# A two-layer graph network on one core: normalising and projecting the first node groups ahead of the rest

## The chip, the cores and the metric

The kernel runs on one core of a Trainium2 chip. The metric is the device time of one launch, in microseconds; of several runs the median is given. Engines are named as in the profile: PE (matrix products and transposes; PEld is its weight load), DVE, ACT and POOL (elementwise engines), and SP, which only issues DMAs. ACT and POOL issue DMAs too, each through a queue of its own; an engine that issues a DMA does nothing else meanwhile.

## The reference, cut to what matters

There are n = 3327 nodes with d = 128 features each, an adjacency matrix of 3327 x 3327, and H = 8.

```
h = relu(layernorm(x))                          # over the 128 features
deg = adj.sum(1);  deg[deg == 0] = 1
g = (adj.T @ h / deg) @ W_n.T + b_n + h @ W_c.T + b_c
x = x + relu(gamma * batchnorm(g) + beta)       # batch norm: over the nodes

h = relu(layernorm(x))
q = (h @ Wq.T).reshape(d, n, H)                 # the same for k and v
a = einsum('dnh,dmh->dnm', q, k) * d**-0.5 + adj + adj
o = einsum('dnm,dmh->dnh', softmax(a, axis=2), v)
x = x + o.reshape(n, H * d) @ Wo.T
```

The reshape to (d, n, H) cuts the row-major result of n x 1024 into 128 batches of 3327 rows with 8 columns. Attention is done on 128 batches, each with 3327 x 3327 scores. One node gives 128 rows, so 104 nodes (13312 rows) cover four batches (13308 rows).

## The kernel before, in words

**Layer 0.** x lies in SBUF as `xs`, 128 partitions x 26 chunks (NC) x 128 features, node c*128+p on partition p. The adjacency comes in 26 blocks of rows; PE gathers them into eight PSUM banks (`acc`, the last block of 512 nodes shorter), while ACT and DVE sum and take maxima. Then follow the division by the degree, the products with `wn`, and the batch-norm statistics, which end in `scale` and `shift`. `A` then holds the layer's value with features on partitions.

**Between the layers** (lines 615 to 722, written out by hand in program order, one list that each engine runs in its own order). `parts` are chunk ranges: part 0 is chunk 0, part 1 chunks 1 to 3, the others four chunks each. For a part, `relu` (ACT, L620) applies batch norm, `residual` turns it with PE (L626) and adds it to `xs` on DVE (L634), `measure` takes layernorm statistics on DVE (L638, L640), `roots` is a square root on ACT (L381), `factors` two small DVE operations that give `rs` and `mr`; `second_norm` (L646, L651) applies them, and `columns` turns the result with PE and takes the relu into `B`, features on partitions (L659, L661). Part 0 is taken through all this first, as the first 104 nodes are projected at once: `projections` with `quick` true makes six parts (k, q, v, two halves of 512 columns each). A projection of k or q is split into a rounded value and its remainder, `o[:, 0]` and `o[:, 1]`, so that products at reduced precision keep their accuracy. Each is stored twice (`L245`, four DMAs for each half, 208 KB each): `qT` and `kT` in DRAM have 4*H = 32 rows, in the order in which a product of 32 rows pairs value and remainder. The other parts follow; at the end all columns go to `hd` in DRAM (L665), and `xs` to `xd` (L722), from where later groups read them.

**Attention** (`attention`, L764). There are 32 groups (NG) of four batches (G). A group has a tile set: `k` and `q` with 32 partitions for each batch, and `v`. `first_loads` fills set 0: k is read from `kT` into the `k` tile of set 1 as a staging area `ks`, four DMAs, two on SP and two on ACT (L943), q's first 512 columns likewise, then adjacency tiles `at` and weight tiles `wt` through `fetch` (L836, L826), then v. Seven copies on ACT, DVE and POOL sort k from the staging order (L956; a chunk's elements are 26 apart there, 104 bytes). The other sets are filled during the group before, by `loads`: k in two halves through a tile `ks`, 14 sorts on POOL (L190), and q.

The queries of a group are cut into seven blocks y. Strings of tokens (WIDE, NARROW, LAST) give the order of work in a block:
- `A` (`plain`): two PE products (L851) into one of three PSUM buffers, and on DVE the sum with the adjacency (L972) into `d`. Four fill one `d` tile.
- `B` (`weighted`): two products, the exponential on ACT into `f` (L991), the product with weights `wt` on POOL (L992).
- `L`: the exponential of a full `d` tile on ACT (L910).
- `v`: eight matmuls with v into `av` (`second`, L725), six tokens behind; here, too, DMAs and small work are put in: `loads`, `more_weights` (group 0 alone: a tile `t` is read at L870, its exponential stored as weights), `further`, and in group 0 the list `others` (q's remaining columns, L1048).
- `P`, `E`: the start and the middle of one part of `extra`: the projections of a later group (through `further`: `hj`, 104 columns, is read from `hd`, L890), or the output of an earlier one (`outputs`, which reads `xj` from `xd`). There are two P in a wide block, 12 in a group.

Pools that are closed leave their space to the pools of attention, in order of address: so the first `f` tile lies on the old `xs`, and its first use waits for the store of `xs`.

Of the kernel before, what the change touches and what calls it, by code (L numbers as in the profile page):

```python
# [18 lines left out]
N = 3327  # L19
# [16 lines left out]
RUN = 4  # L36
HEAVY = (2, 6, 10, 14, 18, 21)
# [19 lines left out]
def tile_two_layer_gnn(  # L57
# [33 lines left out]
    qT = dram.tile([4 * H, TP], F32, name="qT")  # L91
    kT = dram.tile([4 * H, TP], F32, name="kT")
# [7 lines left out]
    xd = dram.tile([P, NC, D], F32, name="xd")  # L100
    hd = dram.tile([P, NP], F32, name="hd")
# [30 lines left out]

    def tile_set(qkp, x):
        k = qkp.tile([P, NC, P], F32R, name=f"k{x}")
        q = qkp.tile([P, NP], F32R, name=f"q{x}")
        v = qkp.tile([P, G, NC, H + 1], F32, name=f"v{x}")

        nc.vector.memset(v[96:, :, NC - 1, :], 0.0)
        return q, k, v
# [4 lines left out]
    def q_load(q, p0, d, n0=0, n=NP):  # L144

        return (
            q[p0 : p0 + 4 * H, n0 : n0 + n].bitcast(F32), qT[:, bass.ds(d * N + n0, n)]
        )

    def k_load(k, p0, d, n0=0, n=NP):  # L150
        return k[p0 : p0 + 4 * H].bitcast(F32), kT[:, bass.ds(d * N + n0, n)]
# [13 lines left out]
    def loads(tiles, d, ksp):  # L165
# [9 lines left out]
        qs = [dma(*q_load(q, 32 * b, batch(b))) for b in range(G)]  # L175
        vv = [dma(*a) for a in v_loads(v, d)]
        todo = []
        for half in range(2):
# [3 lines left out]
                dma(*k_load(ks, 32 * b, batch(b), half * (NP // 2), NP // 2))  # L182
                for b in range(G)
            ]
            todo += vv if half == 0 else []
            for c in range(0, NC, 4):
                n = min(4, NC - c)

                def sort(ks=ks, c=c, n=n, half=half):
                    nc.gpsimd.tensor_copy(  # L190
                        k[:, c : c + n, half * 64 : half * 64 + 64],
                        ks.bitcast(F32).rearrange("g (p c) -> g c p", c=NC)[:, c : c + n, :],
                    )

                todo.append(sort)
                if c % 8 == 4 and qs:
                    todo.append(qs.pop(0))
# [4 lines left out]
    def projection(wk, hj, j, s, e, quick, ov, factor, queue):  # L202
# [8 lines left out]
        if s == 2:  # L211
            nc.vector.tensor_copy(
# [28 lines left out]
        for a in range(2):  # L241
            for i in range(2):
                g = ((a, i), (i, a))[s]
                g = (2 * g[0] + g[1]) * H + e * (H // 2)
                queue[i].dma_start(  # L245
                    (qT, kT)[s][g : g + H // 2, tok].rearrange("g (p u) -> p g u", u=D),
                    of[:CH, a].rearrange("p (h u) -> p h u", u=D),
                )

    def projections(wk, hj, j, quick, ov, factor, queues=((nc.sync, nc.sync),) * 3):  # L250
# [3 lines left out]
        ]  # L254

    def outputs(wk, j):
# [7 lines left out]
        for c in range(j * CH // P, ((j + 1) * CH - 1) // P + 1):  # L264
            m0, m1 = max(j * CH, c * P), min((j + 1) * CH, (c + 1) * P)
            nc.sync.dma_start(
                xj[m0 - j * CH : m1 - j * CH], xd[m0 - c * P : m1 - c * P, c, :]
            )
# [38 lines left out]
    with tc.tile_pool(name="l0", bufs=1) as l0, tc.tile_pool(  # L307
        name="l0adj", bufs=4
    ) as ap, tc.tile_pool(name="l0s", bufs=4) as sp, tc.tile_pool(
        name="l0w", bufs=1  # L310
    ) as lw, tc.tile_pool(name="l0last", bufs=1) as ll, tc.tile_pool(name="l0p", bufs=1, space=PSUM) as pp:


        xs = ll.tile([P, NC, D], F32, name="xs")
        A = l0.tile([P, NC, D], F32, name="A")
        B = ll.tile([P, NC, P], F32, name="B")
        C = l0.tile([P, NC, P], F32, name="C")
        A2, B2, C2 = (t.rearrange("p c d -> p (c d)") for t in (A, B, C))
        junk = l0.tile([P, N], mybir.dt.bfloat16, name="junk")
        deg = l0.tile([P, NC], F32, name="deg")  # L320
        rdeg = l0.tile([P, NC], F32, name="rdeg")
        wn = l0.tile([P, D], F32, name="wn")
        wc = l0.tile([P, D], F32, name="wc")
        cols = l0.tile([P, 4], F32, name="cols")
        bias = l0.tile([P, 1], F32, name="bias")
# [12 lines left out]
        def load(c):  # L338

            a = ap.tile([P, 7 * NB], F32, name="a")  # L340
# [17 lines left out]
        root = l0.tile([P, 1], F32, name="root")  # L358
# [6 lines left out]
        st = l0.tile([P, NC, 6], F32, name="ln_st")  # L365
        mv = l0.tile([P, NC, 2], F32, name="ln_mv")
        sd = l0.tile([P, NC], F32, name="ln_sd")
        rs = l0.tile([P, NC], F32, name="ln_rs")
        mr = l0.tile([P, NC], F32, name="ln_mr")
# [86 lines left out]
        top = l0.tile([P, 1], F32, name="top")  # L456
        b = l0.tile([1, 6], F32, name="bound")
# [45 lines left out]
        for c in range(NC):  # L503
# [17 lines left out]
            def reduce():  # L521
                nc.scalar.activation(  # L522
                    junk, a[:, :N], AF.Copy, accum_out=deg[:, c : c + 1]
# [30 lines left out]
        a = ap.tile([P, 7 * NB], F32, name="a")  # L554
# [7 lines left out]
        bst = l0.tile([P, NQ, 6], F32, name="bn_st")  # L562
        bmv = l0.tile([P, 2], F32, name="bn_mv")
        scale = l0.tile([P, 1], F32, name="bn_scale")
        shift = l0.tile([P, 1], F32, name="bn_shift")
# [63 lines left out]
        def bank_of(i):  # L629
            return acc[max(0, i - 1)]  # L630
# [11 lines left out]
        def second_norm(i, engine=None):  # L642

            for c in range(*parts[i]):
                if engine is None:
                    nc.scalar.activation(  # L646
                        C[:, c, :], xs[:, c, :], AF.Relu,
                        bias=mr[:, c : c + 1], scale=rs[:, c : c + 1],
                    )
                else:  # L650
                    engine.tensor_scalar(  # L651
                        C[:, c, :], xs[:, c, :], rs[:, c : c + 1], mr[:, c : c + 1],
                        ALU.mult, ALU.add,
                    )

        def columns(i, scalar):
            pt, cs = turned_part(i, C, bank_of(i))
            if scalar:
                nc.scalar.activation(B[:, cs, :], pt, AF.Relu)  # L659
            else:  # L660
                nc.vector.tensor_scalar(B[:, cs, :], pt, 0.0, None, ALU.max)  # L661

        def keep_columns(c0, c1):
            cs = slice(c0 * P, c1 * P)
            nc.gpsimd.dma_start(hd[:, cs], B2[:, cs])  # L665

# [4 lines left out]
        roots(0, 1)  # L671
        factors(0, 1)
        second_norm(0, nc.vector)
        columns(0, True)
        relu(2)
        now = projections(
            sp, B2[:, :CH], 0, True, ov, low_half[:CH, 1:2],
            ((nc.scalar, nc.gpsimd), (nc.sync, nc.gpsimd), (nc.gpsimd,)),
# [14 lines left out]
        residual(1)  # L693
        project(1)
        relu(3)
        measure(1)
        multiply(2, 3)
        residual(2)
        project(2)
        measure(2)  # L700
        project(3)
        relu(4)
        multiply(4, 5)
        relu(5)
        relu(6)
        relu(7)
        project(4, 5)
        for i in range(3, len(parts)):
            residual(i)
            measure(i)  # L710
        roots(1, NC)

        nc.scalar.activation(root, eps, AF.Exp)
        factors(1, NC)
        for i in range(1, len(parts)):
            second_norm(i, (nc.vector, nc.gpsimd, None)[i % 3])
        for i in range(1, len(parts)):
            columns(i, i % 3 != 0)
            if i == 4:
                keep_columns(0, 16)  # L720
        keep_columns(16, NC)
        nc.gpsimd.dma_start(xd, xs)  # L722

# [40 lines left out]
    def attention():  # L764
# [3 lines left out]
        with tc.tile_pool(name="exd", bufs=3) as ep, tc.tile_pool(  # L768
            name="qk1", bufs=1
        ) as qkp1, tc.tile_pool(name="adj", bufs=4) as ap, tc.tile_pool(  # L770
            name="adw", bufs=3
        ) as wp, tc.tile_pool(name="exf", bufs=6) as fp, tc.tile_pool(
# [8 lines left out]
            for av in avs2:  # L781
                nc.vector.memset(av, 0.0)
# [61 lines left out]
            def product(i, y, c, half):  # L844
                q, k, _ = sets[i % 2]
                n0, w = qblocks[y]
# [13 lines left out]
                q_load(sets[0][0], 32 * b, b, NB, NP - NB) for b in range(G)  # L860
            ]

            def more_weights(i, y, v):

                if i or y + 1 >= NY or v not in (2, 16, 24):
                    return
                n0, w = qblocks[y + 1]
                if v == 2:
# [12 lines left out]
            extra, begun, then = [], [], []  # L881

            def further(i, y, v):

                if v == 6:
                    for j in [1, 2] if i == 0 else [i + 2] if i + 2 < NG else []:
                        if y != (2 * (j - 1) if i == 0 else 0):
                            continue
                        hj = wk.tile([P, CH], F32, name="hj")
                        nc.sync.dma_start(hj, hd[:, j * CH : (j + 1) * CH])  # L890
                        extra.extend(projections(wk, hj, j, False, ov, low_half[:CH, 1:2]))
# [44 lines left out]
            def first_loads():  # L936

                q, k, v = sets[0]
                ks = sets[1][1].rearrange("p c n -> p (c n)")
                for load, tile_, n in ((k_load, ks, NP), (q_load, q, NB)):  # L940
                    for b in range(G // 2):
                        for x, queue in ((b, nc.sync), (b + 2, nc.scalar)):
                            queue.dma_start(*load(tile_, 32 * x, x, 0, n))  # L943
                fetch(0, 4)
                fetch(1, 0)
# [3 lines left out]
                for c, copy in (  # L949
                    (16, nc.scalar.copy), (0, nc.vector.tensor_copy),  # L950
                    (4, nc.gpsimd.tensor_copy), (8, nc.scalar.copy),
                    (20, nc.vector.tensor_copy), (12, nc.gpsimd.tensor_copy),
# [306 lines left out]
```

## Time and profile before

| | us |
|---|---|
| median of 3 runs | 9930.07 (9927.71 to 9933.09) |
| the profiled execution | 9923.27 |
| its span, first to last instruction | 9921.5 |
| PE, DVE, ACT, POOL busy | 9328.9, 9260.4, 9762.9, 8406.5 |
| mean granted PE clock | 0.994 |

Busy shares are means over the whole span. The layers differ: layer 0 ends at about 212 us, attention runs from about 262 us to the end, and what lies between is short and has limits of its own. Sums by stretch and the timelines of single engines tell more of it than the page.

### The profile page before, as it was taken

To read this page: it belongs to the slowest core of one execution; us is meant where nothing else is said; L and a number is where in the kernel's file an instruction comes from. 1 tells how busy PE (TensorE), PEld (TensorE's weight loads), DVE (VectorE), ACT (ScalarE), POOL (GpSimd) and SP (SyncE) were. 2 spreads that over 40 slices of the span, in tenths; PEclk is the share of its full clock that TensorE was granted. 3 is DMA by queue.
4 is the path that set the end of the run, shared out by engine and by line. 5 is a ranking of instruction groups with operands and counts; after the bars stand their busy time and mean duration, and the time that the engine had idled before them with its cause. 6 is when DMAs were issued, how large, how long until landed. Compare 5 with 4: busy or idle time off the path is not lost. (4 is left out here: it accounts for less than half of the span.)

```text
span 9921.5 us, 180311 instructions
## 1 busy us (share of the span) xinstructions
PE 9328.9 (94%) x71535; PEld 2846.0 (29%) x71535; DVE 9260.4 (93%) x8949; ACT 9762.9 (98%) x5375; POOL 8406.5 (85%) x4084
## 2 busy tenths in 40 slices
PE   7899999999999999999999999999999999999998
PEld 3222222222222222222222222222222222222222
DVE  5899999999999999999999999999999999999998
ACT  5999999999999999999999999999999999999999
POOL 2788888888888888888888888888888888888887
PEclk9999999999999999999999999999999999999999
DMA  7765556665566665566655566655566656666554
GB/s 302 219 194 174 176 173 185 179 180 172 172 181 186 180 177 171 174 181 183 181 176 174 173 184 181 181 175 172 175 184 184 179 167 176 179 185 181 164 158 130
DMA packets 1132126, 1789.64 MB, mean 180 GB/s; under 512 B 95558, under 2 KB 464196, under 8 KB 1121924
## 3 DMA queue, kind: packets, MB, share of 16 engines
q1 hardware_dynamic: 1127071, 1760.22, 59.7%
q8 instruction: 561, 9.19, 0.4%
q10 hardware_dynamic: 2772, 12.06, 0.3%
q0 software_dynamic: 1424, 5.73, 0.2%
q14 instruction: 298, 2.43, 0.1%
HBM read 1620.90 MB, written 156.76 MB: 179 GB/s over the span
## 5 line engine op out<-in xcount | busy, mean ns | idle before, releaser
L972 DVE SCALAR_TENSOR_TENSOR d<-at,s 128x1024 f32<-128x1024 f32 x7488 | 8693.6, 1216 | 509.3 <-PE s L851 255.7
L992 POOL TENSOR_TENSOR f<-f,wt 128x1024 f32<-128x1024 f32 x3328 | 7875.6, 2395 | 1273.8 <-ACT f L991 1270.0
L910 ACT ACTIVATE d<-d 128x4096 f32<-128x4096 f32 (+1 forms) x1888 | 6931.6, 3671 | 1.3 <-DVE av L743 0.4
L851 PE MATMUL s<-q,k 32*128 32x512 f32 x23296 | 3939.7, 464 | 488.8 <-ACT f L991 261.7
L725 PE MATMUL av<-d,v 128*9 128x512 f32 x32256 | 3810.2, 565 | 33.5 <-ACT d L910 33.4
L991 ACT ACTIVATE f<-s 128x1024 f32<-128x1024 f32 x3328 | 3385.4, 1094 | 15.8 <-PE s L851 8.9
L851 PEld LDWEIGHTS s<-q,k 32*128 32x128 f32 x23296 | 1776.4, 182 | 4950.7 <-DVE d L972 2826.3
L725 PE MATMUL av<-f,v 128*9 128x512 f32 x14336 | 1749.1, 564 | 0.2 <-issue 0.2
L725 PEld LDWEIGHTS av<-d,v 128*9 128x9 f32 x32256 | 576.8, 89 | 1288.2 <-issue 1044.1
L725 PEld LDWEIGHTS av<-f,v 128*9 128x9 f32 x14336 | 266.2, 89 | 578.4 <-issue 414.1
L190 POOL CAST k<-ks 128x256 fp32r<-128x256 f32 x434 | 286.7, 661 | 0.0
L516 PE MATMUL acc<-a,A 128*128 128x512 f32 (+1 forms) x364 | 159.1, 589 | 26.0 <-DMA a<-in_adj 26.0
L237 POOL TENSOR_TENSOR o<-pf,o 104x512 fp32r<-104x512 f32 x124 | 160.1, 1291 | 9.9
L735 DVE STREAM_TRANSPOSE avs<-av 128x512 f32<-128x512 f32 (+1 forms) x224 | 150.4, 672 | 2.7 <-PE av L725 2.7
L494 POOL TENSOR_SCALAR heavy<-heavy 128x3328 f32<-128x3328 f32 x6 | 17.8, 2960 | 137.0 <-DMA heavy<-in_adjT 112.8
L525 DVE TENSOR_REDUCE amax<-a 128x1 f32<-128x3327 f32 x26 | 93.6, 3604 | 39.4 <-DMA a<-in_adj 39.4
L522 ACT ACTIVATE junk<-a 128x3327 bf16<-128x3327 f32 x26 | 77.3, 2973 | 29.9 <-DMA a<-in_adj 27.8
L516 PEld LDWEIGHTS acc<-a,A 128*128 128x128 f32 x364 | 71.1, 199 | 116.0 <-issue 95.2
L236 POOL CAST o<-pf 104x512 fp32r<-104x512 f32 x124 | 76.2, 615 | 0.0
L285 PE MATMUL av<-wo,t 128*104 128x128 f32 x512 | 72.4, 286 | 0.0
L206 PE MATMUL av<-wq,hj 128*104 128x512 f32 x124 | 70.4, 650 | 0.0
L206 PE MATMUL av<-wv,hj 128*104 128x512 f32 x124 | 69.5, 643 | 0.0
(138 smaller groups left out, 841.5 us busy)
## 6 DMA issues: line engine op xcount, KB each, us to landing
at<-in_adjT SPq DMA_DIRECT2D x1856, 512.0 KB
wt<-wd SPq DMA_DIRECT2D x1664, 256.0 KB
kT<-o SPq DMA_DIRECT2D x252, 208.0 KB
qT<-o SPq DMA_DIRECT2D x248, 208.0 KB
ks<-kT SPq DMA_DIRECT2D x248, 208.0 KB
q<-qT SPq DMA_DIRECT2D x124, 416.0 KB
a<-in_adj SPq DMA_DIRECT2D x26, 1663.5 KB
v<-ov SPq DMA_DIRECT2D x31, 468.0 KB
```

What stands on the lines that cost most here:

```text
L190: nc.gpsimd.tensor_copy(k[:, c : c + n, half * 64 : half * 64 + 64], ks.bitcast(F32).rearrange("g (p c) -> g c p", c=NC)[:, c : c + n, :],)
L206: nc.tensor.matmul(bank[:CH], hj, wqk[s][:, e * NB : (e + 1) * NB], start=True, stop=True)
L237: nc.gpsimd.tensor_tensor(o[:CH, 1], f[:CH], of[:CH, 0], ALU.subtract)
L516: nc.tensor.matmul(acc[i][:, :w], A[:, c, :], a[:, n0 : n0 + w], start=(c == 0), stop=(c == NC - 1),)
L525: nc.vector.tensor_reduce(amax[:, c : c + 1], a[:, :N], AX.X, ALU.max, apply_absolute_value=True)
L725: nc.tensor.matmul(av[32 * b : 32 * b + H + 1, :w], tiles[2][:, b, c, :], e, start=first, stop=last,)
L735: nc.vector.transpose(avs[:, :J, :].rearrange("p j h -> p (j h)"), av[:, : 32 * J].rearrange("p (q j) -> p j q", j=J),)
L851: nc.tensor.matmul(p[:, x, e * w : (e + 1) * w], k[rs, c + e, :], q[rs, n0 : n0 + w], start=True, stop=True,)
L910: nc.scalar.activation(flat, flat, AF.Exp, scale=2.0)
L972: nc.vector.scalar_tensor_tensor(d[:, z], have[0, i, y, j // 4][:, j // 2 % 2] .unsqueeze(1).to_broadcast([P, 2, QB]), SAFE / 2, p, ALU.mi ...
L991: nc.scalar.activation(f, p, AF.Exp, scale=2.0)
L992: nc.gpsimd.tensor_tensor(f, f, have[1, i, y, j // 2].unsqueeze(1).to_broadcast([P, 2, QB]), ALU.mult,)
```

## The change

The DRAM tensors `qT` and `kT` hold 16 rows instead of 32: each half is stored once for the value and once for the remainder (two DMAs instead of four). `q_load` reads a batch in three pieces (16, 8 and 8 rows), `k_load` in two of 16 rows; so the repetition is made in reading.

Between the layers only nodes 0 to 207 get the second normalisation there: chunk 0 on DVE, chunk 1 on POOL, each followed by a transpose and a relu into `B`. Nodes 0 to 103 are projected as before, the columns of nodes 104 to 207 go to `hd`, which is now that small. `second_norm`, `columns` and `keep_columns` are gone. `rs` and `mr` become two more columns of `xs` (now `xf`, D + 2 wide) and are stored with it in `xd`. From group 2 on, `columns_of` reads a group's rows with their factors, scales them on POOL, and as one more part of `extra` turns them on PE and takes the relu on DVE.

The reads of k and of q's first columns move from `first_loads` to a place ahead of the last `roots`. The staging tile (set 1's `k`) is allocated at the start. The first six products read k from the staging tile, 104 bytes from element to element; three sorts (two on ACT, one on POOL) stay at the start, four go to POOL within the list `others`. The q stores of the first group move from ACT's queue to SP's, two copies of v from DVE to ACT, and pools change their order, so that `adj` and `adw` lie on layer 0's first tiles. The clearing of the two `av` banks moves behind the first products.

```diff
-    qT = dram.tile([4 * H, TP], F32, name="qT")       # kT alike
+    qT = dram.tile([2 * H, TP], F32, name="qT")
...
     def q_load(q, p0, d, n0=0, n=NP):
-        return (
-            q[p0 : p0 + 4 * H, n0 : n0 + n].bitcast(F32), qT[:, bass.ds(d * N + n0, n)]
-        )
+        return [
+            (
+                q[p0 + p : p0 + p + r, n0 : n0 + n].bitcast(F32),
+                qT[g : g + r, bass.ds(d * N + n0, n)],
+            )
+            for p, g, r in ((0, 0, 2 * H), (2 * H, H, H), (3 * H, 0, H))
+        ]
     def k_load(k, p0, d, n0=0, n=NP):
-        return k[p0 : p0 + 4 * H].bitcast(F32), kT[:, bass.ds(d * N + n0, n)]
+        return [
+            (k[p0 + p : p0 + p + 2 * H].bitcast(F32), kT[:, bass.ds(d * N + n0, n)])
+            for p in (0, 2 * H)
+        ]
...
         for a in range(2):
-            for i in range(2):
-                g = ((a, i), (i, a))[s]
-                g = (2 * g[0] + g[1]) * H + e * (H // 2)
-                queue[i].dma_start(
+            g = a * H + e * (H // 2)
+            queue[a].dma_start(
...
+    def columns_of(wk, j):
+        xt = wk.tile([P, D + 2], F32, name="xt", bufs=1)
+        rows(xt, j, D + 2)
+        hj = wk.tile([P, CH], F32, name="hj", bufs=1)
+        def scaled():
+            nc.gpsimd.tensor_scalar(
+                xt[:CH, :D], xt[:CH, :D], xt[:CH, D : D + 1], xt[:CH, D + 1 :],
+                ALU.mult, ALU.add,
+            )
+        def turn():
+            bank = yield
+            nc.tensor.transpose(bank[:, :CH], xt[:CH, :D], ident[:CH, :CH])
+            yield
+            nc.vector.tensor_scalar(hj, bank[:, :CH], 0.0, None, ALU.max)
+            yield
+        return hj, scaled, turn()
...
         now = projections(
             sp, B2[:, :CH], 0, True, ov, low_half[:CH, 1:2],
-            ((nc.scalar, nc.gpsimd), (nc.sync, nc.gpsimd), (nc.gpsimd,)),
+            ((nc.sync, nc.gpsimd), (nc.sync, nc.gpsimd), (nc.gpsimd,)),
         )
...
-        roots(1, NC)
+        ks = ks2[1].rearrange("p c n -> p (c n)")
+        for load, tile_, n in ((k_load, ks, NP), (q_load, sets[0][0], NB)):
+            for d in range(G):
+                queue = (nc.sync, nc.scalar)[d // 2]
+                for args in load(tile_, 32 * d, d, 0, n):
+                    queue.dma_start(*args)
+        roots(4, NC)
         nc.scalar.activation(root, eps, AF.Exp)
-        factors(1, NC)
-        for i in range(1, len(parts)):
-            second_norm(i, (nc.vector, nc.gpsimd, None)[i % 3])
-        for i in range(1, len(parts)):
-            columns(i, i % 3 != 0)
-            if i == 4:
-                keep_columns(0, 16)
-        keep_columns(16, NC)
-        nc.gpsimd.dma_start(xd, xs)
+        factors(4, NC)
+        nc.gpsimd.dma_start(xd, xf)
...
                 q, k, _ = sets[i % 2]
+                if i == y == 0 and sum(number) <= FRESH:
+                    k = sets[1][1].rearrange("p c n -> p (c n)").rearrange(
+                        "g (p c) -> g c p", c=NC
+                    )
...
-                for c, copy in (
-                    (16, nc.scalar.copy), (0, nc.vector.tensor_copy),
-                    (4, nc.gpsimd.tensor_copy), (8, nc.scalar.copy),
-                    (20, nc.vector.tensor_copy), (12, nc.gpsimd.tensor_copy),
-                    (24, nc.vector.tensor_copy),
-                ):
+                for c, copy in (
+                    (0, nc.scalar.copy), (16, nc.gpsimd.tensor_copy),
+                    (4, nc.scalar.copy),
+                ):
+                    sort(c, copy)
+                for z, c in enumerate((20, 8, 12, 24)):
+                    others.insert(3 * z, lambda c=c: sort(c, nc.gpsimd.tensor_copy))
```

## The prediction

> **What bounds the kernel now.** I read the page's busy times and costliest groups first, then the sums by stretch, then the timelines of the DMA queues and of ACT in the stretch that the change rewrites.
>
> ```profile
> PE 9328.9 (94%) x71535; PEld 2846.0 (29%) x71535; DVE 9260.4 (93%) x8949; ACT 9762.9 (98%) x5375; POOL 8406.5 (85%) x4084
> L972 DVE SCALAR_TENSOR_TENSOR d<-at,s 128x1024 f32<-128x1024 f32 x7488 | 8693.6, 1216 | 509.3 <-PE s L851 255.7
> L992 POOL TENSOR_TENSOR f<-f,wt 128x1024 f32<-128x1024 f32 x3328 | 7875.6, 2395 | 1273.8 <-ACT f L991 1270.0
> L910 ACT ACTIVATE d<-d 128x4096 f32<-128x4096 f32 (+1 forms) x1888 | 6931.6, 3671 | 1.3 <-DVE av L743 0.4
> L991 ACT ACTIVATE f<-s 128x1024 f32<-128x1024 f32 x3328 | 3385.4, 1094 | 15.8 <-PE s L851 8.9
> ```
> ACT's two exponentials have almost no idle time ahead of them: 1.3 and 15.8 us in the whole run. The sums by stretch (length, then PE, PEld, DVE, ACT, POOL busy, clock, DMA share, GB/s) show where ACT does idle:
>
> ```profile
> 0.00:212.00 212.00, 180.16 (x443) 82.61 (x443) 124.70 (x160) 127.00 (x121) 42.69 (x51) 0.97 0.82 329
> 212.00:267.50 55.50, 20.58 (x72) 12.50 (x72) 28.32 (x94) 17.74 (x34) 16.23 (x23) 0.63 0.74 214
> 267.50:580.00 312.50, 293.13 (x2124) 83.39 (x2124) 283.04 (x267) 303.54 (x168) 263.55 (x132) 0.95 0.69 203
> 580.00:9860.00 9280.00, 8793.46 (x68456) 2648.84 (x68452) 8790.29 (x8391) 9277.10 (x5036) 8051.99 (x3866) 1.00 0.60 177
> ```
> From 580 to 9860 us ACT is busy for 9277.10 of 9280 us, and the change takes no exponential away; nothing is to be won there. The edits meet the path in the 55.5 us from 212.00 to 267.50, in which ACT works 17.74 us. There the timeline of SP's queue (start, length, instruction) and that of ACT show this:
>
> ```profile
> 219.61 2.84 SPq L245 DMA_DIRECT2D kT<-o  x4
> 239.83 1.27 SPq L943 DMA_DIRECT2D k<-kT  x2
> 245.10 0.78 SPq L943 DMA_DIRECT2D q<-qT  x2
> ```
> ```profile
> 225.66 10.47 ACTq L245 DMA_DIRECT2D qT<-o  x2
> 236.18 2.71 ACT L620 ACTIVATE A<-A,bn_shift,bn_scale 128x512 f32<-128x512 f32 x4 [10.55 <-DMA qT<-o]
> 251.73 0.84 ACTq L943 DMA_DIRECT2D k<-kT  x2
> 261.39 2.29 ACT L956 CAST k<-k 128x512 fp32r<-128x512 f32 x2 [9.51 <-DMA hd<-B]
> 267.50 1.02 ACT L991 ACTIVATE f<-s 128x1024 f32<-128x1024 f32 x1 [3.82 <-DMA xd<-xs]
> 270.66 3.62 ACT L910 ACTIVATE d<-d 128x4096 f32<-128x4096 f32 x1 [0.19 <-DVE d L972]
> ```
> The path of this stretch is: k stored (219.6), landed and read back by SP (239.8), but ACT's half of the reads only at 251.7, because ACT first hangs 10.47 us in the issue of two q stores, then finishes the BN relu, the second norm and the columns of all 26 chunks. Those reads land at 261.4, the sorting starts, the first f waits for the xd store until 267.5, and the first large exponential starts at 270.66. That last time is my mark: from it on ACT is nearly full, so what it moves, the end moves.
>
> **The change, part by part.** Up to the BN shift at 212.87 us nothing that counts is different.
>
> B's first columns: the relu that writes them now stands behind the residual and statistics of chunks 1 to 3 (DVE 0.55 + 0.67 + 0.30 us) and a root (0.29), part of it under the relu of chunks 4 to 7, which moves ahead. Start 216.52 becomes about 217.8, a loss of 1.3 us.
>
> Stores: q and k go out in 8 DMAs instead of 16. In 220 to 240 us the three queues moved 2.16, 0.85 and 0.76 MB, in all 3.77 MB of 16 x 0.213 + 0.48 (v), about 0.19 MB per us. Now it is 8 x 0.213 + 0.48 + 0.05 (hd) = 2.24 MB, so 12 us from about 221.5 on, with k's 0.85 MB first. The k stores should have landed at about 230, the last q store at 234 to 237. Bounds for k: 227 (0.19 MB per us, nothing beside it) and 236 (the present SP tail: issued by 222.4, not read before 239.8). I take 230, nearer to the rate, since half of the bytes are gone. None of the stores is on ACT's queue any more, so the 10.47 us hang goes; relus 4 to 7 end at about 228 instead of 238.9, two v copies of 0.6 us on ACT included (they were DVE's). The last statistics on DVE end at about 235 instead of 244.6.
>
> Reads: 8 k DMAs of 0.213 MB and 12 small q DMAs, half on SP, half on ACT, now ahead of the last root. ACT waits here for stores and, as completion semaphores are used again, in the built program some q issues also wait until a k read has landed. Queued behind them on ACT: the root of chunks 4 to 25, the Exp table load (1.28), the two sorts and the first f; for the root wait DVE's factors and POOL's xd store. SP's 0.85 MB of k took 5 us (240.1 to 245.1), ACT's 9.7 us beside hd and xd. For 1.7 MB on both queues beside the end of the q stores I take 8 us (bounds 6 and 13): k there at 238, q at about 241.5, ACT free of issues at about 242. On SP the first at and wt follow, landing at about 243.
>
> Removed: the second norm of 25 chunks (POOL 4.16, ACT 3.17, DVE 2.19 us side by side), 25 transposes and their columns, 5.5 us of chain from 246.2 to 251.7, and 1.6 of the 1.7 MB of hd. The wait of the first f for xd goes, as f no longer lies on xs; it moves to the first t load on SP (L870 before), which holds SP until xd has landed. xd is issued at about 244 and took 14.3 us; behind the t load stand the third wt and the fifth at, needed some 13 us after the first f. That just fits; if not, 2 to 4 us.
>
> First products: 6 products read k strided from its staging tile, so they need no sort. The sort's cast shows a strided read: 1.198 us on ACT for 128x512, against 0.56 us for a plain copy of that size (L412). A weight load of 182 ns might so become 0.4 us, which hides under the other matmul of the pair; bounds for the four products of the first exponential 0 and 4 us, taken 0.5. The Trainium skill's page "SBUF — State Buffer" (section "Door 1: The DMA port swizzle") speaks against this edit: reads that go to a new 16-byte line at each element pay a penalty, and here each element is 104 bytes from the next. No row shows PE doing it; by the page alone I would take the upper end.
>
> Ramp: ACT has root 0.3, table 1.3, Exp 0.2 and two sorts of 1.2 from 242 on, so f at about 246.5. DVE makes the first four d in 4 x 1.2 us from 243.5 on, the fourth product waiting for the PSUM of the first f. First large exponential at 250, against 270.66: 20.7 us won. The two av memsets (1.03 us) now follow the fourth d; four POOL sorts of 1.7 us come between the f of group 0. POOL idles 49 us of 312.5 there, so I put them at 0, with up to 4 us if PE waits for f.
>
> Groups 1 to 31: hj is no longer read but made. Each of 30 groups adds on POOL one 128-element scaling (0.47 us by L651), one transpose (0.38 by L626), one DVE relu (about 0.35), and on SP 8 issues net (16 k and 12 q reads instead of 8 and 4, 8 stores fewer) of 0.45 us. ACT gets nothing. Cover: POOL idles 1228 us and DVE 490 us in 580 to 9860, and SP waits 2507 us for POOL's f. Cost 0; without cover 30 x 0.47 = 14 us. The page "DMA: Bandwidth & Descriptors" (section "Why a DMA increments its semaphore by 16 and not by 1") says that a DMA is spread over the largest number up to 16 that divides its outer sizes, so an 8-row q read would use 8 engines; no row shows this, and by it these reads would take about twice as long, an estimate.
>
> Sum against the profiled execution: 9923.27 (span 9921.50 and 1.77 around it) - 20.7 = 9902.6. The median of the runs lies 6.8 us above it, 9930.07, and becomes 9909.4.
>
> **The rivals.** A measurement of this kernel tells about 0.2%, 20 us, from no change; the forecast lies on that edge.
> - Reads queue up (gain 5 to 15): the q stores' small packets on SP's queue crawl as SP's k stores do now (0.85 MB from 219.6 to 239.8); the last k reads wait for them, q for these, and ACT, stuck in its issues, holds root, table and sorts. Reads 6 us later and f with them: mark at 258, time 9917. For it: the 20 us that SP's stores take. Against: POOL's queue has 0.8 MB less beside them.
> - Everything runs free (gain 25 to 31): k landed at 227, reads in 6 us, mark at 244: time 9903. For it: at loads reach 0.36 MB per us at 248 to 252.
> - Slower: each group's chain xt read, POOL scaling, PE transpose stalls PE. In group 0 at 357.20 ACT waited 2.41 us for PE, which waited for POOL's o. At that price 30 groups cost 72 us: time 9930 - 21 + 72 = 9981. It decides from 1.4 us a group on (41 / 30). Against: groups 1 to 31 have the same kind of part 6 times each, and ACT loses 2.9 us in all.
> - The staging of less data wins nothing, since another transfer (at, wt, v) sets the first product: they could be issued only behind the q reads, so this is part of the first rival.
>
> **How the numbers follow.** Forecast (mark moves 16 to 25 us) 0.5, a little over half of it beyond 20 us; reads queue up 0.2; free 0.2; slower 0.1, nearly all of it over 0.2%. Faster 0.28 + 0.2 = 0.48; same 0.22 + 0.2 + 0.01 = 0.43; slower 0.09. The range takes the main case, most of the free one (gain 31: 9899) and of the queue (gain 8: 9922).
>
> **What would show it.** Right: the first large exponential at 246 to 255 us; k stores read back at about 230; no DMA issue of 10 us on ACT; ACT full from 580 us on as now. Wrong: k or q reads issued after 240, ACT's roots behind them after 246, a t load that holds SP beyond 260, or ACT idle time in the groups, released by PE or POOL.

## The result, and the profile after

The changed kernel takes 10010.82 us (median of 6 runs, 10005.15 to 10014.6), against 9933.1 us for the kernel before in the same session (6 runs). The ratio is 1.0078, 95% interval 1.0065 to 1.0091: it is slower by some 78 us, where 20.7 us less were forecast. The span of the profiled execution grew by more, from 9921.5 to 10009.4 us, because the profiled execution of before (9923.27 us) ran 10 us below the median of its kernel.

Page of the changed kernel: engine totals, then the groups that answer to those shown of before (line, engine, operation | busy us, mean ns | idle us just before them, and what ended most of it).

```profile
PE 9351.2 (93%) x71541; PEld 2830.5 (28%) x71541; DVE 9262.0 (93%) x8966; ACT 9773.6 (98%) x5366; POOL 8409.2 (84%) x4104
...
L1010 DVE SCALAR_TENSOR_TENSOR d<-at,s 128x1024 f32<-128x1024 f32 x7488 | 8696.6, 1216 | 606.5 <-PE s L879 348.7
L1030 POOL TENSOR_TENSOR f<-f,wt 128x1024 f32<-128x1024 f32 x3328 | 7873.9, 2395 | 1367.4 <-ACT f L1029 1356.5
L946 ACT ACTIVATE d<-d 128x4096 f32<-128x4096 f32 (+1 forms) x1888 | 6918.9, 3665 | 1.7 <-DVE d L1010 0.8
...
L1029 ACT ACTIVATE f<-s 128x1024 f32<-128x1024 f32 x3328 | 3375.3, 1089 | 104.0 <-PE s L879 97.9
...
L287 PE MATMUL av<-ident,xt 104*128 104x104 f32 x30 | 9.8, 328 | 79.4 <-POOL xt L280 79.4
```

The two exponentials are as long as before, but ACT now idles 104.0 us ahead of the smaller one, where it idled 15.8. What ends that idle time is PE (97.9 us). The last row is new: the transpose of `columns_of`, 30 times, and PE sits idle 79.4 us ahead of it until POOL has scaled `xt`. Thirty operations that are busy for 9.8 us hold their engine up for eight times as long.

Sums by stretch of the changed kernel (length, then PE, PEld, DVE, ACT, POOL busy, granted clock, DMA share, GB/s):

```profile
212.00:267.50 55.50, 28.25 (x112) 11.23 (x113) 34.00 (x96) 28.19 (x34) 21.34 (x17) 0.63 0.71 203
267.50:580.00 312.50, 287.08 (x2175) 82.26 (x2171) 281.49 (x267) 301.02 (x165) 263.52 (x135) 0.97 0.66 189
580.00:9860.00 9280.00, 8730.70 (x67761) 2611.23 (x67757) 8706.42 (x8333) 9192.04 (x4982) 7978.45 (x3860) 0.99 0.61 170
```

In the first stretch ACT works 28.19 us instead of 17.74, the gain that was aimed at. In the last it works 9192.04 of 9280 us, where 9277.10 were full: 85 us are lost there. Timeline of SP's queue, then of ACT, at the start of attention:

```profile
229.76 5.15 SPq L743 DMA_DIRECT2D k<-kT  x4
236.77 5.89 SPq L743 DMA_DIRECT2D q<-qT  x6
```
```profile
229.77 5.15 ACTq L743 DMA_DIRECT2D k<-kT  x4
239.35 4.75 ACTq L743 DMA_DIRECT2D q<-qT  x6
244.15 0.31 ACT L417 ACTIVATE ln_sd<-ln_mv,eps 128x22 f32<-128x22 f32 x1 [14.46 <-DMA q<-qT]
...
248.94 1.02 ACT L1029 ACTIVATE f<-s 128x1024 f32<-128x1024 f32 x1 [0.86 <-ACT k L984]
...
252.84 3.62 ACT L946 ACTIVATE d<-d 128x4096 f32<-128x4096 f32 x1 [0.37 <-DVE d L1010]
```

k is read back at 229.8 on both queues, ACT is free of its issues at 244.15, and the mark, the first large exponential, stands at 252.84 (270.66 before). Now one of the later groups: POOL's own timeline, then PE, then ACT (start, length, instruction, and in brackets the idle time just before and its releaser).

```profile
934.45 7.06 POOL L1030 TENSOR_TENSOR f<-f,wt 128x1024 f32<-128x1024 f32 x3 [0.60 <-ACT f L1029]
941.48 0.46 POOL L280 TENSOR_SCALAR xt<-xt 104x128 f32<-104x128 f32 x1
```
```profile
941.99 0.31 PE L287 MATMUL av<-ident,xt 104*128 104x104 f32 x1 [2.65 <-POOL xt L280]
942.23 0.51 PE L879 MATMUL s<-q,k 32*128 32x512 f32 x4
942.67 3.57 PE L751 MATMUL av<-d,v 128*9 128x512 f32 x16
946.17 0.73 PE L879 MATMUL s<-q,k 32*128 32x512 f32 x6
```
```profile
940.38 3.75 ACT L946 ACTIVATE d<-d 128x4096 f32<-128x4096 f32 x1
947.00 1.02 ACT L1029 ACTIVATE f<-s 128x1024 f32<-128x1024 f32 x1 [2.87 <-PE s L879]
```

The rows of `xt` were asked for at 919.0; they are not late. The scaling of 0.46 us is late, because it stands in POOL's queue behind three products `f` that take 7.06 us. PE reaches its transpose 2.65 us too early and executes in order, so the products behind the transpose wait too.

Then PE is slow as well. Its granted clock (1.00 is full speed) is 1.00 from 940 to 942 us, 0.50 from 943 to 946, and 1.00 again from 947. The sixteen products with v that stand behind the transpose take 3.57 us; in e1 below the same sixteen take 1.90 us, at a clock of 1.00. ACT's next f needs the products s behind these sixteen and comes 2.87 us late. The wait happens once in each of 30 groups, and each time at least 3.4 us at half clock go with it. Behind group 0 PE spends 109 us at half clock, against 7 us before. No run separates what the wait alone costs from what the slower clock adds to it.

The span can be cut at the mark, 309.3 us behind it (group 0, about) and 421 us before the end. ACT's idle time in the two middle parts, by the same cuts for every kernel told of below ("from BN" is the mark less the start of the root for `bn_scale`, which takes out that layer 0 ended up to 3 us earlier or later). The columns in us are of one profiled execution each. The kernels were measured in different sessions, in which before took 9924 to 9933 us, so each ratio is to before in the same session:

| kernel | mark (from BN) | ACT idle in group 0 | in the groups behind | mark to end | ratio to before, interval |
|---|---|---|---|---|---|
| before | 270.66 (58.9) | 7.8 | 2.9 | 9650.8 | |
| after | 252.84 (39.3) | 12.9 | 87.5 | 9756.6 | 1.0078 [1.0065, 1.0091] |
| e1, scaling at token 7 | 254.77 (40.3) | 12.6 | 5.5 | 9659.4 | 0.9992 [0.9983, 1.0002] |
| e2, hj from hd | 252.43 (39.8) | 12.3 | 3.4 | 9663.1 | 0.9986 [0.9976, 0.9995] |
| e3, scaling later | 251.51 (40.0) | 14.6 | 186.4 | 9860.8 | 1.0189 [1.0172, 1.0206] |
| e4, stored once alone | 281.37 (68.0) | 13.4 | 2.6 | 9655.8 | 1.0014 [1.0004, 1.0023] |
| e5, e1 with FRESH = 0 | 253.32 (39.9) | 12.5 | 7.7 | 9667.0 | 0.9991 [0.9982, 1.0000] |
| e6, e1, reads on POOL | 252.44 (40.3) | 12.5 | 3.3 | 9659.3 | 0.9988 [0.9979, 0.9997] |
| e7, e1, reads on SP | 254.90 (42.5) | 12.4 | 4.6 | 9662.0 | 0.9986 [0.9977, 0.9995] |
| e8, repeated in one DMA | 269.81 (57.8) | 30.2 | 18.8 | 9700.2 | 1.0038 [1.0024, 1.0052] |
| e9, e1, stored twice | 260.24 (47.7) | 8.9 | 0.5 | 9648.8 | 0.9980 [0.9971, 0.9989] |

From the mark to the end the changed kernel needs 105.7 us more than before: 84.6 us of idle time behind group 0, 5.1 in group 0, 1.1 at the end, and 15 us in which ACT is busy longer over the same number of instructions (one by one they are no longer, but they overlap less with their neighbours). Less the 17.8 us of the mark this is the 88 us by which the span grew.

### The profile page after: what moved, and what is told of

Read it like the earlier page. It is cut to its first block, busy times and chain, and to the rows that moved or that the text cites. A ratio compares the mean times of both kernels' runs of the same rounds, so it can differ in the third digit from the quotient of the medians.

```text
span 10009.4 us, 180861 instructions
## 1 busy us (share of the span) xinstructions
PE 9351.2 (93%) x71541; PEld 2830.5 (28%) x71541; DVE 9262.0 (93%) x8966; ACT 9773.6 (98%) x5366; POOL 8409.2 (84%) x4104
## 5 line engine op out<-in xcount | busy, mean ns | idle before, releaser
L751 PE MATMUL av<-d,v 128*9 128x512 f32 x32256 | 3857.6, 571 | 35.4 <-ACT d L946 34.3
L1029 ACT ACTIVATE f<-s 128x1024 f32<-128x1024 f32 x3328 | 3375.3, 1089 | 104.0 <-PE s L879 97.9
L530 POOL TENSOR_SCALAR heavy<-heavy 128x3328 f32<-128x3328 f32 x6 | 17.8, 2960 | 137.7 <-DMA heavy<-in_adjT 137.7
L287 PE MATMUL av<-ident,xt 104*128 104x104 f32 x30 | 9.8, 328 | 79.4 <-POOL xt L280 79.4
L772 DVE TENSOR_TENSOR oq<-avs,av 128x128 f32<-128x128 f32 (+1 forms) x224 | 62.2, 278 | 7.6
## 6 DMA issues: line engine op xcount, KB each, us to landing
ks<-kT SPq DMA_DIRECT2D x496, 104.0 KB
q<-qT SPq DMA_DIRECT2D x248, 104.0 KB
```

The lines of the kernel that those rows point to most:

```text
L751: nc.tensor.matmul(av[32 * b : 32 * b + H + 1, :w], tiles[2][:, b, c, :], e, start=first, stop=last,)
L1029: nc.scalar.activation(f, p, AF.Exp, scale=2.0)
```

## The experiments

**e1: the scaling two tokens earlier.** It is given to POOL at token 7 instead of 9, which is the 8th `v` of the block instead of the 10th.

```diff
-                if v == 9 and scaling:
+                if v == 7 and scaling:
```

> The changed kernel with the scaling of a later group's rows given to POOL at the 8th v of block 1 instead of the 10th, so that it stands ahead of three f products on POOL (7.1 us) that it stood behind. Theory W (PE's transpose waits for POOL's scaling, 2.65 us in each of 30 groups, and ACT loses 2.9 us or a little more for it): the wait on xt falls to 0, ACT idles under 0.5 us in a later group, and the time is 10011 - 30 x 2.9 to 3.4 = 9909 to 9924. Rival R (the reads of k and q in more and smaller DMAs, 28 instead of 12 a group, hold SP and starve the products): time stays at 10005 to 10015. Rival P (one more part for PE and DVE in each group is what costs): 9995 to 10011.

Measured: 9914.52 us, ratio 0.9992 [0.9983, 1.0002]. Page of this kernel, and POOL's timeline in the group shown above:

```profile
L1029 ACT ACTIVATE f<-s 128x1024 f32<-128x1024 f32 x3328 | 3390.0, 1096 | 19.1 <-PE s L879 16.5
```
```profile
931.71 0.45 POOL L280 TENSOR_SCALAR xt<-xt 104x128 f32<-104x128 f32 x1
932.33 9.43 POOL L1030 TENSOR_TENSOR f<-f,wt 128x1024 f32<-128x1024 f32 x4 [0.17 <-ACT f L1029]
```

The same 0.45 us now stand ahead of the long run of products, and the transpose (at 937.15) finds `xt` ready. At half clock PE now spends 11 us behind group 0 instead of 109. Nothing else in the program differs, and from the mark to the end 97.1 us are saved. By the ratios, each to before in its own session, the saving is 0.86%, or about 85 us; so the scaling cost 2.8 to 3.2 us in each of the 30 groups. The whole loss is the place of the scaling in POOL's queue; neither the smaller reads nor the added part costs anything of that size. What is left of the change is within 0.2% of before.

**e2: no scaling, no transpose.** The groups read `hj` from `hd` again, always the same 104 columns, so the second norm of nodes 208 on is left out of the computation.

```diff
-                        hj, scaled, turn = columns_of(wk, i + 2)
-                        scaling.append(scaled)
-                        extra.append(turn)
+                        hj = wk.tile([P, CH], F32, name="hj", bufs=1)
+                        nc.sync.dma_start(hj, hd)
```

> The changed kernel without scaling, transpose and relu in the groups: every later group projects the columns of nodes 104 to 207 from hd again (it leaves out the normalisation of nodes 208 on). Reads of k and q as changed. W and P: 9905 to 9924, P alone with a clear distance to the kernel that scales earlier. R: 10005 to 10015.

Measured: 9910.22 us, 0.9986 [0.9976, 0.9995], idle time behind group 0 of 3.4 us. It agrees with e1 within the intervals: once in time, the scaling, transpose and relu of 30 groups cost at most a few us.

**e3: the scaling later.** It is given just ahead of the transpose.

```diff
-                if v == 9 and scaling:
-                    scaling.pop(0)()
...
                         elif token == "P":
                             if extra:
+                                if scaling:
+                                    scaling.pop(0)()
```

> The changed kernel with the scaling given to POOL only just ahead of the transpose, behind one f product more (2.4 us). W: PE's wait on xt grows from 2.65 to about 5 us, ACT's loss by 2.0 to 2.4 us in each of 30 groups, time 10071 to 10083. R and P: 10005 to 10015.

Measured: 10111.1 us, 1.0189 [1.0172, 1.0206], more than expected. Page of this kernel:

```profile
L1027 ACT ACTIVATE f<-s 128x1024 f32<-128x1024 f32 x3328 | 3369.6, 1086 | 202.7 <-PE s L879 195.8
...
L287 PE MATMUL av<-ident,xt 104*128 104x104 f32 x30 | 12.9, 431 | 147.5 <-POOL xt L280 147.5
```

PE waits 4.9 us a group instead of 2.65, about one product of 2.4 us more, but from mark to end each group costs 3.5 us more (104.2 / 30). The sign and the mechanism are as expected; the size is not. What the expectation left out is the clock: PE spends 270 us at half clock behind group 0, against 109 us in the changed kernel, in most groups 6.8 us instead of 3.4. The sixteen products with v take 3.51 us on average where e1 has 1.90. That this makes up the rest of the loss is likely, but no run shows it alone.

**e4: storing once alone.** The kernel before, with `qT` and `kT` of 16 rows, half of the stores, and reads in three and two pieces; nothing else of the change.

```diff
-    qT = dram.tile([4 * H, TP], F32, name="qT")       # kT, q_load, k_load as in the change
+    qT = dram.tile([2 * H, TP], F32, name="qT")
```

> The kernel before with one part of the change alone: q and k are stored once, and read in three and two pieces. Its q stores stay on ACT's queue. W: ACT stays full in the later groups, and the stretch before attention gains some of the 20 us: 9915 to 9930. R: ACT idles 2.5 to 3 us a group, time 9995 to 10020.

Measured: 9937.81 us, 1.0014 [1.0004, 1.0023], slower than before and outside what was expected. SP reads k back at 228.50 (239.83 before), so the stores do land earlier, and ACT's issues of q stores no longer hang. But ACT's timeline shows why nothing comes of it:

```profile
246.38 14.90 ACTq L950 DMA_DIRECT2D k<-kT  x4
266.11 6.91 ACTq L950 DMA_DIRECT2D q<-qT  x6
273.12 2.23 ACT L963 CAST k<-k 128x512 fp32r<-128x512 f32 x2 [26.51 <-DMA q<-qT]
```

ACT reaches its ten reads at 246.38, earlier than its four before (251.73), but hangs 26.5 us in issuing them, where 9.5 us went by before. The mark comes 10.7 us later (9.1 from BN). In the old order of the work the reads in pieces cost more than the halved stores save. The stores of `hd` and `xd` (issued from 245.0 on) run beside these reads, and which of them holds the reads up was not separated.

**e5: no strided products.** e1, and all first products wait for sorted k (`FRESH` is the number of first products that read the staging tile).

```diff
-FRESH = 6
+FRESH = 0
```

> The kernel with the earlier scaling, and all products wait for the sorted k (no strided first products). Theory S (the strided first products save a wait for the sorts): the first large exponential 3 to 4 us later than with them. Rival Q (q's last read, which the trace shows landing after five products could have started, sets the first d whatever k's form): 0 to 1.5 us later. Time against the earlier scaling alone: S +3 to +4, Q 0 to +1.5 us.

Measured: 9914.47 us, 0.9991 [0.9982, 1.0000]; the mark is 39.9 us behind BN, as in e1 (40.3). The strided read saves nothing that shows, and costs nothing either. PE's weight loads of the first products, by form (x count | busy us, mean ns | idle before), in the changed kernel from 244 to 249 us, then in e5 from 244 to 250:

```profile
L879 PEld LDWEIGHTS s<-q,k 32*128 32x128 f32 x7 | 1.1, 300 | 4.5 <-DMA q<-qT 3.5 <-issue 1.1
```
```profile
L879 PEld LDWEIGHTS s<-q,k 32*128 32x128 f32 x8 | 1.3, 289 | 16.6 <-ACT k L984 15.4 <-DVE d L1010 1.2
```

Loads with 104 bytes from element to element take 300 ns, from sorted k 289 ns, 4% more; the granted clock is 0.50 in both. The rule of the Trainium skill's page "SBUF — State Buffer" (section "Door 1: The DMA port swizzle"), a penalty for each access that goes to a new 16-byte line, spoke against this edit. PE's weight load shows no more of it than these 4%, and the measurement decides.

**e6 and e7: who issues the first reads.** e1, with ACT's half of the k and q reads on POOL's queue (e6), or all of them on SP's (e7).

```diff
-                queue = (nc.sync, nc.scalar)[d // 2]
+                queue = (nc.sync, nc.gpsimd)[d // 2]        # e6; e7: queue = nc.sync
```

> The kernel with the earlier scaling, and the half of the reads of k and q that ACT issued goes to POOL's queue. Theory A (ACT stands 14.3 us in the issue of its ten reads, and root, table, sorts and first f behind them set the start): ACT's root at about 235 instead of 244, first large exponential at about 248 instead of 253 to 255, time 5 to 7 us shorter. Rival D (the reads themselves, q's landing above all, set the start): first large exponential within 1.5 us of what it was, time the same.

> The kernel with the earlier scaling, and all 20 reads of k and q on SP. A: ACT is free, but the q reads are issued one after the other behind the k reads, whose completion semaphores are used again: start 0 to 4 us later than with ACT's half. D: 3 to 8 us later, since one queue moves all reads.

Measured: 9911.13 us, 0.9988 [0.9979, 0.9997], and 9912.72 us, 0.9986 [0.9977, 0.9995]. ACT's timeline in e6:

```profile
235.73 0.32 ACT L417 ACTIVATE ln_sd<-ln_mv,eps 128x22 f32<-128x22 f32 x1 [6.06 <-DVE ln_mv L676]
...
243.75 2.24 ACT L984 CAST k<-k 128x512 fp32r<-128x512 f32 x2 [6.19 <-DMA k<-kT]
248.54 1.02 ACT L1029 ACTIVATE f<-s 128x1024 f32<-128x1024 f32 x1 [2.55 <-issue]
```

ACT is free 8.5 us earlier than in e1 (23.6 against 32.1 us behind BN), and then waits for k; the first f starts 36.4 us behind BN in both. So ACT's 14.5 us of issuing lay beside the landing of the reads, and it is the reads that set the start. With all reads on SP the mark comes 2.2 us later than on two queues. That is less than the 3 to 8 us which D expected of e7 and lies in A's range, so it is e6 that decides for D.

**e8: the repetition inside one DMA.** e6, each batch read by one k DMA and two q DMAs whose source repeats by a step of zero, in place of pieces.

```diff
-            (k[p0 + p : p0 + p + 2 * H].bitcast(F32), kT[:, bass.ds(d * N + n0, n)])
-            for p in (0, 2 * H)
+            k[p0 : p0 + 4 * H].bitcast(F32),
+            kT[:, bass.ds(d * N + n0, n)].unsqueeze(0).to_broadcast([2, 2 * H, n]),
```

> As the kernel with POOL's queue, and each repetition is made inside one DMA by a source dimension of step 0: one read of k and two of q for a batch instead of two and three (8 and 8 a group instead of 16 and 12). Theory N (the number of reads costs: in group 0 ACT idles 12 to 13 us in every kernel that stores once, against 7.8 before): idle time of group 0 back to 8 to 9 us, time 4 to 6 us below that of the kernel with POOL's queue. Rival O (the order of the work at the start, a DVE that begins later or earlier, makes the idle time): idle time stays at 12 to 13 us, time within 2 us.

Measured: 9962.1 us, 1.0038 [1.0024, 1.0052]. DMA issues of e6, then of e8, 226 to 262 us (count, KB each, median us from issue to landing):

```profile
k<-kT POOLq DMA_DIRECT2D x4, 208.0 KB, 10.0
```
```profile
k<-kT POOLq DMA_DIRECT2D x2, 416.0 KB, 26.1
```

One read of 416 KB lands after 26.1 us, where each of the two that it replaces lands after 10.0, and the mark comes 17.4 us later. The Trainium skill's page "DMA: Bandwidth & Descriptors" (section "Why a DMA increments its semaphore by 16 and not by 1") says that a DMA runs on the largest number of engines up to 16 that divides its outermost sizes; with an outermost size of two that would be two. The row agrees in direction, but it does not show how many engines worked, and other DMAs of POOL's queue, which repeat nothing, land later too (the v store after 14.9 us instead of 7.6). With such reads nothing can be said on group 0's idle time, for which this run was meant too.

**e9: stored twice, in the new order.** e1 with the 32 rows of before, 16 stores and one read for each batch.

```diff
-            for p, g, r in ((0, 0, 2 * H), (2 * H, H, H), (3 * H, 0, H))
+            for p, r in ((0, 4 * H),)                    # k_load alike, stores as before
```

> The first experiment (scaling at token 7), with one part of the change undone: q and k are stored twice again (4*H rows each, 16 store DMAs instead of 8, on SP's and POOL's queues) and each batch is read back in one DMA (k 4, q 4 at the start, 2 and 2 of them on ACT, instead of 8 and 12). This asks what storing once is worth at the start, and where ACT's 5 us of extra idle time in group 0 (7.8 us before, 12.3 to 13.4 in every kernel that stores once) come from. Theory N (the reads in pieces do it: more DMAs and more issues in group 0's loads): ACT's idle time in the 309 us after the mark falls back to about 8 us. Theory O (it comes from what the start leaves over, the transposed relu and the order of the first products, not from the pieces): it stays at 12 to 13 us. For the start, theory S (stores set it): the k stores carry twice the bytes, SP reads k back at 236 to 240 instead of 230, and the mark (first large exponential) comes 6 to 10 us later than the 254.8 us of the first experiment, 261 to 265. Theory H (ACT's hang in issuing ten reads sets it): with four reads on ACT the hang shrinks by more than the stores cost, and the mark stays at 252 to 257. Time: N and S 9915 to 9919, N and H 9907 to 9911, O and S 9920 to 9925, O and H 9912 to 9916.

Measured: 9911.32 us against 9932.13 in its own session, 0.9980 [0.9971, 0.9989]; no other kernel here has a lower ratio, though its interval overlaps those of e1, e2, e5, e6 and e7. SP's queue, then ACT:

```profile
240.69 2.85 SPq L745 DMA_DIRECT2D k<-kT  x2
```
```profile
249.95 0.31 ACT L419 ACTIVATE ln_sd<-ln_mv,eps 128x22 f32<-128x22 f32 x1 [19.83 <-DMA k<-kT]
...
260.24 3.62 ACT L948 ACTIVATE d<-d 128x4096 f32<-128x4096 f32 x1 [0.37 <-DVE d L1012]
```

The stores do set the start (theory S in substance, the mark 0.8 us under its bounds): SP reads k back 10.7 us later than in e1, and the mark comes 7.4 us later from BN. But ACT's idle time in group 0 falls back from 12.6 to 8.9 us (theory N), and mark to end is 10.7 us shorter. The time itself, 9911.32 us, lies under the 9915 to 9919 us that N and S together expected. So in these two executions storing once wins 7.4 us ahead of the mark, and the reads in pieces give them back behind it. Which of the pieces' properties does this (their number, their rows, or the issues on SP) was not separated.

## Why the prediction was wrong

The step that failed is one term: "Groups 1 to 31 ... Cover ... Cost 0; without cover 30 x 0.47 = 14 us". It set POOL's 0.47 us against POOL's 1228 us of idle time. But idle time is cover only for work that may wait until the engine is idle. Here PE waits for this work at a given place, POOL executes in order, and ahead of it stood up to three products of 2.4 us. The cost is the time that PE stands at the transpose (2.65 us), with the half clock behind it: 85 to 97 us in all, six to seven times the bound "without cover". e1 shows the term alone: the same work, put earlier, costs nearly nothing, so the forecast of 0 would have been right for that place.

The slower rival named exactly this chain and priced it from a row of before (2.41 us a group, 9981 us). It was given a chance of 0.1 because "groups 1 to 31 have the same kind of part 6 times each, and ACT loses 2.9 us in all". That argument compares unlike things: in the kernel before, no idle time of PE in a group ends with POOL (one does in the whole run, 6.0 us between the layers). And the row was misread. The f that starts at 357.20 reads a product s that ended at 357.11, and PE, which made it, had not waited for POOL: it worked without a gap from 353.21 on, at a granted clock of 0.50 until 356. The row shows a slow PE, not the chain of the rival. The order written out in the changed kernel (scaling at token 9, behind it the `P`) would have told how many products stand between; it was not counted. The rival's price, 2.41 us a group, was low but near (2.8 to 3.2 measured); since its row shows another wait, that is in part luck.

The other steps, in their order:

- **The transition**, 20.7 us forecast: 17.8 by the mark, 19.6 counted from BN. Right. k was to be read back at 230 (229.8), ACT free of issues at 242 (244.15), the first f at 246.5 (248.94), the mark at 250 (252.84), of which 1.7 us are a later end of layer 0.
- **The reads as rival** ("ACT, stuck in its issues, holds root, table and sorts"): ACT was stuck for 14.5 us, but e6 shows that this hid behind the landing of the reads. A sign of being wrong did come true, since the last q reads were issued after 240, without the loss that it stood for.
- **The t load held by xd** "just fits": it went out at 256.49. In e1 it went out at 259.34 and in e6 at 251.98, with the same idle time of ACT in group 0 (12.6 and 12.5 us), so the hold cost nothing that shows.
- **The strided products**, 0.5 us taken: nothing (e5). That a sort fewer saved as little is because q, not k, landed last.
- **Stores halved**: k was read back when forecast, and e9 puts the part of the stores at 7.4 us. But the reads in pieces were put at 0 and cost about as much. The forecast looked for their price in q reads of 8 rows and did not add one.
- **Group 0's added POOL sorts and av memsets**, 0 with up to 4: ACT idles 5.1 us more there. It is not these: e4 has none of them and idles 13.4, e9 has them all and idles 8.9. What the kernels that idle longer share is the reads in pieces.

Taken together, with the scaling in time the change would have been worth 9 us by medians (e1) and not 20.7: the transition gives 18 to 20, and about 9 of it are lost again behind the mark, most likely to the pieces.

## What to carry to other kernels

When an engine that executes in order is given work that another engine waits for, count what stands ahead of it in its own queue at that moment, up to the place where the other engine needs it; the engine's idle time over the run says nothing on this. Put such work ahead of the long operations, as early as its data are there: here two tokens decided 85 to 97 us. And look at the granted clock behind a stall of PE: here the stall took speed from PE afterwards too, and the engine that it feeds lost a little more than the stall itself (2.87 us for 2.65).

## What the runs showed of the hardware

- With each wait of PE of 2.65 us came at least 3.4 us at a granted clock of 0.50, in all 30 groups, and in e3, with waits of 4.9 us, 6.8 us in 27 of 30. In e1, without the wait, the clock stays at 1.00 there and sixteen products take 1.90 us in every group; in the changed kernel they take 3.41 us on average.
- Delaying one 0.46 us operation of POOL by one more product of 2.4 us (e3) cost 3.5 us a group from the mark to the end.
- An engine that issues many reads can hang in them: ACT 14.5 us over ten reads in the changed kernel, 26.5 us over ten in e4. Whether it costs anything depends on what else could run (nothing in e1, as e6 shows).
- A PE weight load of 32x128 whose elements are 104 bytes apart takes 300 ns against 289 ns, at a granted clock of 0.50.
- A read of 416 KB on POOL's queue that repeats its source in an outermost dimension of two landed after 26.1 us, where plain reads of 208 KB landed after 10.0.
